# Aggregating four batches at once: 49 two-level Strassen products with a streamed right operand in place of 26 products on pairs

## The chip, the core and the metric

The kernel runs on one core of one Trainium2 chip, all in fp32. The metric is the device time of one execution in microseconds (us). Three runs of the kernel before gave 1821.66, 1821.86 and 1822.44 us, a median of 1821.86.

## What is computed

There are 16 batches of 1024 nodes with 128 features, and one 1024 x 1024 matrix `adj` that all of them share. Layer 0 is one graph convolution and layer 1 is five steps of a gated unit. Both take the normalized and rectified input and add their result to the residual.

```python
# layer 0
h = relu(layernorm(x));  x = x + adj @ (h @ W) + bias
# layer 1
h = relu(layernorm(x))
for _ in range(5):
    m  = adj @ h                       # the aggregation
    av = concat([m, m])
    u3 = h @ u3_w.T + u3_b
    z  = sigmoid(av @ w3_w.T + w3_b + u3)
    r  = sigmoid(av @ w4_w.T + w4_b + u3)
    hv = tanh(av @ w5_w.T + w5_b + (r * h) @ u5_w.T + u5_b)
    h  = (1 - z) * h + z * hv
x = x + h
```

`in_matrix` and `out_matrix` are the same matrix, so the two halves of each weight are added once and one aggregation per step is enough. The heavy parts are the aggregation (1024 x 1024 times 1024 x 128 for each batch, once in layer 0 and five times in layer 1) and the **gates** (five 128 x 128 products on 1024 columns for each batch and step).

## The kernel before

Batches go in eight **pairs**. Two pairs are in flight in layer 1, and their steps alternate: aggregation of one pair, its gates, aggregation of the other pair, its gates. While one pair is aggregated, the other's hidden state, which the gates leave transposed (features by nodes), is turned into natural order: two 32 x 32 block transposes on VectorE (`squares_to_dram`, L591), a store to DRAM (`fn<-sq`) and four loads for each batch (`natural_from`, `hN<-fn`), all issued from the SP queue (L183).

The aggregation of a pair (`aggregate`, products at L435) cuts `adj` into 4 x 4 blocks of 256 x 256 and the pair into 4 x 2 blocks. Instead of 32 block products it forms 26. Each product is two matmuls of 128x128 weights on 256 columns, since one block has two chunks of 128 nodes. The right operands of all 26 are sums of blocks of `adj`; they are made once, at the start (`adj_sums`, L279 to L284), and stay in SBUF in `right_op` for the whole program. The left operands (`forms`, L407 to L411) are sums of blocks of the pair and are made for each aggregation on VectorE and ScalarE. Products are accumulated in four PSUM banks (b1 to b4); ScalarE copies banks out (`pair_of` L447, `one_of` L452) and VectorE adds the copies into `mT`, the transposed result (L459, L462).

The layer 0 aggregations of pairs 0 and 1 are done without the scheme (`aggregate_plainly`, L554), with 512-column matmuls. The other six pairs' layer 0 work, called the prelude, runs as a background of layer 1: small pieces are put between products by `place(k)`, and the pair's aggregation takes the turn of one step. `po` (L675) is layer 0's product with W.

The gates (`gates`, L714 to L755) work on four units of 512 columns in a pair: for each unit two matmuls into a bank, a sigmoid, then a third matmul into the same bank and a second sigmoid, then two matmuls into another bank and a tanh. `pr` are the banks of the sigmoids, `pv` those of the tanh.

The order of instructions on every engine is the order in which the program is written (`pin`). DMAs all go through `dma` on SP.

Of the kernel before, what the change touches and what calls it, by code (L numbers as in the profile page):

```python
# [43 lines left out]
EARLY = (  # L44
    ("=p3", "p3"),
    ("=p2", "p2"),
    ("a3", "q3", "+", "q4"),
    ("a9", "p3", "+", "a3"),
    ("a10", "p2", "-", "a3"),
    ("a1", "q1", "-", "q3"),  # L50
    ("a7", "p3", "-", "a1"),
    ("a2", "q1", "+", "q2"),
    ("a8", "p2", "+", "a2"),
    ("a4", "q1", "+", "q4"),
    ("=q4", "q4"),
    ("a13", "p4", "+", "a9"),
)
LATE = (
    ("a6 a5", "p23", "+", "q23"),
    ("a15", "p1", "+", "a8"),  # L60
    ("a18", "p4", "+", "a15"),
    ("a16", "a18", "-", "a2"),
    ("a17", "a16", "+", "a1"),
    ("=p1", "p1"),
    ("=p4", "p4"),
    ("a19", "q4", "+", "a18"),
    ("a14", "p1", "-", "a7"),
    ("a11", "q2", "+", "a3"),
    ("a12", "a13", "+", "a10"),
)  # L70
FORM = {a: i for i, a in enumerate(" ".join(f[0] for f in EARLY + LATE).split())}

PRODUCTS = (
    ("T", "=p3", 1, 0),
    ("U", "=p2", 1, 1),
    ("V", "a9", 2, 0),
    ("W", "a10", 2, 1),
    ("X", "a3", 3, 0),
    ("R", "a7", 1, 0),
    ("S", "a8", 1, 1),  # L80
    ("D1", "a4", 4, 0),
    ("D2", "=q4", 4, 0),
    ("O", "a13", 3, 0),
    ("Y", "a1", 1, 0),
    ("Z", "a2", 1, 1),
    ("M", "a5", 2, 0),
    ("N", "a6", 2, 1),
    ("J", "a16", 4, 0),
    ("K", "a17", 1, 0),
    ("L", "a18", 1, 1),  # L90
    ("A1", "=p1", 3, 0),
    ("A2", "=p4", 3, 0),
    ("F", "a19", 4, 0),
    ("H", "a14", 1, 0),
    ("I", "a15", 1, 1),
    ("E", "a11", 2, 0),
    ("G", "=q4", 2, 1),
    ("B", "a12", 1, 0),
    ("C", "=p4", 1, 1),
)  # L100
RIGHT = {p[0]: i for i, p in enumerate(PRODUCTS)}
OPENS = {"T": 1, "V": 2, "X": 3, "D1": 4, "J": 4, "F": 4}

RIGHT_SUMS = (
    ("N", "R24", "-", "R14"),
    ("Z", "R21", "-", "R24"),
    ("T", "R31", "-", "R34"),
    ("B", "R32", "+", "R33"),
    ("G", "R44", "-", "R34"),
    ("S", "N", "-", "R21"),  # L110
    ("t0", "R13", "+", "R14"),
    ("J", "R12", "+", "t0"),
    ("t1", "R23", "+", "R24"),
    ("K", "J", "-", "t1"),
    ("H", "t1", "-", "t0"),
    ("t2", "R31", "+", "R33"),
    ("R", "H", "-", "t2"),
    ("Y", "R", "-", "R12"),
    ("t3", "R12", "+", "R32"),
    ("M", "t3", "-", "R42"),  # L120
    ("t4", "K", "+", "B"),
    ("W", "t4", "-", "R22"),
    ("O", "R42", "-", "t4"),
    ("U", "W", "+", "R21"),
    ("X", "W", "m", "R34"),
    ("V", "O", "-", "R34"),
    ("A2", "R41", "-", "O"),
    ("F", "O", "+", "R43"),
    ("L", "t1", "-", "F"),
    ("I", "R14", "-", "L"),  # L130
    ("t5", "t1", "-", "R44"),
    ("C", "R43", "-", "t5"),
    ("t6", "R11", "+", "S"),
    ("D1", "t6", "-", "R"),
    ("D2", "A2", "-", "D1"),
)
SINGLES = (("A1", 0, 0), ("E", 1, 1))
# [3 lines left out]


ANY, BLOCK, HOLD = range(3)
FREE = (6, 8, 11, 13, 17, 20, 24)
PLAIN = ((0, 0), (1, 1), (0, 1), (1, 0))
UNITS = ((1, 0), (1, 1), (0, 0), (0, 1))
# [3 lines left out]
def tile_two_gnn_layers(  # L150
# [17 lines left out]
    pairs = B // 2  # L168
# [3 lines left out]
    nat = ctx.enter_context(tc.tile_pool(name="nat", bufs=4))  # L172
    flip = ctx.enter_context(tc.tile_pool(name="flip", bufs=2))
    tr = ctx.enter_context(tc.tile_pool(name="tr", bufs=6))
    agg = ctx.enter_context(tc.tile_pool(name="agg", bufs=1))
# [15 lines left out]
    def load_x(b, xt=None, parts=((0, NC),)):  # L191
        xt = xt or x_tile(b)
        for cs in parts:
            cs = slice(*cs)
            dma(xt[:, cs], by_slots(x[b])[:, cs])
        return xt
# [8 lines left out]

    right_op = const.tile([P, len(PRODUCTS), SB, BLK], F32, tag="right", name="right_op")
    forms = const.tile([P, len(FORM), SB, D], F32, tag="forms", name="forms")


    raw = [[None] * NH for _ in range(NB)]  # L210

    def load_adj(i, g, t=None):
        if g == 0 and t is None:
            t = nat.tile([P, N], F32, tag="hN", name=f"raw_{i}")
        elif g == 1:
            first = len(FORM) - (NB - i) * 2 * SB
            t = forms[:, first : first + 2 * SB].rearrange("p s j d -> p (s j d)")
        raw[i][g] = t.rearrange("p (c n) -> p c n", c=SB)
        parts = SB if (i, g) == (0, 0) else 1
        for k in range(parts):  # L220
            cs = bass.ts(k, SB // parts)
            dma(raw[i][g][:, cs], adjT[:, bass.ts(i, SB), bass.ts(g, HALF)][:, cs])

    gb = const.tile([P, D], F32, tag="gb", name="gb")
    w_sb = const.tile([P, 9, D], F32, tag="w", name="w_sb")
    b_sb = const.tile([P, 5], F32, tag="b", name="b_sb")
    xts = {0: load_x(0, parts=((0, 2), (2, CH), (CH, NC))), 1: x_tile(1)}
# [3 lines left out]


    def other_loads(k):
        if k == 0:
            pin(nc.vector.memset(xts[1][:, 0, 0:1], 0.0))
            load_x(1, xts[1])
            load_adj(2, 0)
            return
        if k == 1:
            raw_3 = nat.tile([P, N], F32, tag="hN", name="raw_3")  # L240
            pin(nc.vector.memset(raw_3[:, 0:1], 0.0))
            load_adj(3, 0, raw_3)
            return
        first = len(FORM) - NB * 2 * SB
        pin(nc.vector.memset(forms[:, first, 0, 0:1], 0.0))
        for i in range(NB):
            load_adj(i, 1)
        for b in range(2, 4):
            xts[b] = load_x(b)
        for name, i, j in SINGLES:  # L250
            dma(right_op[:, RIGHT[name]], adjT[:, bass.ts(i, SB), bass.ts(j, BLK)])
        dma(gb, gbias.to_broadcast([P, D]))
        dma(w_sb, weights)
        dma(b_sb, biases)
# [6 lines left out]
    between = {}  # L261

    def adj_sums(first, last):
        def operand(name):
            if name in RIGHT:
                return right_op[:, RIGHT[name]]
            if name in between:
                return between[name]
            i, j = int(name[1]) - 1, int(name[2]) - 1
            return raw[i][j // 2][:, :, bass.ts(j % 2, BLK)]  # L270

        for dst, a, op, b in RIGHT_SUMS[first:last]:
            if dst not in RIGHT:
                tag = "rz"[len(between) % 2]
                t = work.tile([P, HALF], F32, tag=tag, name=f"between_{dst}")
                between[dst] = t.rearrange("p (c n) -> p c n", c=SB)
            o = operand(dst)
            if op == "+":
                pin(nc.vector.tensor_add(o, operand(a), operand(b)))  # L279
            elif op == "-":  # L280
                pin(nc.vector.tensor_sub(o, operand(a), operand(b)))
            else:
                pin(
                    nc.vector.scalar_tensor_tensor(  # L284
                        o, operand(a), -1.0, operand(b), ALU.mult, ALU.subtract
                    )
                )
# [7 lines left out]
    def weight_sums():  # L295
        for wa, wb in ((W3A, W3B), (W4A, W4B), (W5A, W5B)):
            pin(nc.vector.tensor_add(w_sb[:, wa, :], w_sb[:, wa, :], w_sb[:, wb, :]))
        pin(nc.vector.tensor_sub(w_sb[:, W3A, :], w_sb[:, W3A, :], w_sb[:, W4A, :]))
        for i, (ba, bb) in enumerate(((B3, BU3), (B4, BU3), (B5, BU5))):
            pin(nc.vector.tensor_add(bsum[:, i : i + 1], b_sb[:, ba : ba + 1], b_sb[:, bb : bb + 1]))  # L300
        pin(nc.vector.tensor_scalar_mul(nb3, bsum[:, 0:1], -1.0))

    def normalize(dst, src, nm, then, in_parts=False):

        stats, mv, ve, rstd, nmr = {}, {}, {}, {}, {}
        every, first, second = range(NC), range(CH), range(CH, NC)

        def statistics(i, cs):  # L310
            if i not in stats:
                stats[i] = small.tile([P, NC, 6], F32, tag="stats", name=f"stats_{nm}{i}")
            for c in cs:
                pin(nc.vector.bn_stats(stats[i][:, c, :], src[i][:, c, :]))

        def scales(i, cs=every):
            if i not in mv:
                mv[i] = small.tile([P, NC, 2], F32, tag="mv", name=f"mv_{nm}{i}")
                ve[i] = small.tile([P, NC], F32, tag="ve", name=f"ve_{nm}{i}")
# [629 lines left out]
    for piece in todo:  # L949
        piece()  # L950
# [39 lines left out]
```

## Time and profile before

| | before |
|---|---|
| median of three runs | 1821.86 us |
| the profiled execution | 1821.55 us |
| its span, first to last instruction | 1819.8 us |
| TensorE (PE) busy | 1812.6 us, 100% of the span |
| VectorE (DVE) busy | 1391.5 us, 76% |
| ScalarE (ACT) busy | 759.0 us, 42% |
| GpSimd (POOL) busy | 124.8 us, 7% |
| moved by DMA | 145.15 MB, 80 GB/s on average |
| mean granted TensorE clock | 1.000 |

Busy time is the time in which an engine executes an instruction. The profile counts a matmul in fp32 as two records, so 6810 records on PE are about half as many matmuls. A TensorE record's duration is modelled at its end; the spacing of two starts is the better measure of what a matmul costs. DMA-issuing instructions don't count as busy time of the engine that issues them.

### The profile page before, as it was taken

To read this page: it belongs to the slowest core of one execution; us is meant where nothing else is said; L and a number is where in the kernel's file an instruction comes from. 1 tells how busy PE (TensorE), PEld (TensorE's weight loads), DVE (VectorE), ACT (ScalarE), POOL (GpSimd) and SP (SyncE) were. 2 spreads that over 40 slices of the span, in tenths; PEclk is the share of its full clock that TensorE was granted. 3 is DMA by queue.
4 is the path that set the end of the run, shared out by engine and by line. 5 is a ranking of instruction groups with operands and counts; after the bars stand their busy time and mean duration, and the time that the engine had idled before them with its cause. 6 is when DMAs were issued, how large, how long until landed. Compare 5 with 4: busy or idle time off the path is not lost.

```text
span 1819.8 us, 20644 instructions
## 1 busy us (share of the span) xinstructions
PE 1812.6 (100%) x6810; PEld 1273.2 (70%) x6810; DVE 1391.5 (76%) x3266; ACT 759.0 (42%) x1487; POOL 124.8 (7%) x169
## 2 busy tenths in 40 slices
PE   9999999999999999999999999999999999999999
PEld 4666877677766687668766678666866677776666
DVE  6887877687788786878778877777878777766777
ACT  3445354435335334543434533553344333334433
POOL 4211002000002000200000200020000000000000
PEclk9999999999999999999999999999999999999999
DMA  4231132112631113111352111311153312111123
GB/s 165 88 121 47 47 92 71 46 47 76 196 111 58 47 47 116 47 47 47 112 178 93 58 58 36 116 47 55 39 160 106 105 58 75 54 46 47 47 70 116
DMA packets 87803, 145.15 MB, mean 80 GB/s; under 512 B 9744, under 2 KB 65168, under 8 KB 87696
## 3 DMA queue, kind: packets, MB, share of 16 engines
q1 hardware_dynamic: 87696, 143.83, 25.1%
q8 instruction: 54, 0.88, 0.2%
q14 instruction: 53, 0.43, 0.1%
HBM read 77.73 MB, written 66.06 MB: 79 GB/s over the span
## 4 chain that ended last, share of the span: by engine, by line
PE 98%; DVE 2%; DMA 0%; issue 0%; ACT 0%; DVEq 0%
PE pr L714 23%; PE bT L435 22%; PE pv L714 15%; PE bV L435 11%; PE bX L435 7%; PE bD L435 4%; PE bT_a L435 3%; PE pq_a L554 3%; PE bJ L435 2%; PE bF L435 2%; PE bV_a L435 2%; PE po L675 2%; PE bX_a L435 1%; PE bD_a L435 1%; DMA raw<-in_adjT_dram 0%; PE bJ_a L435 0%
## 5 line engine op out<-in xcount | busy, mean ns | idle before, releaser
L435 PE MATMUL bT<-right_op,forms 128*128 128x256 f32 x1920 | 455.0, 379 | 0.0
L435 PEld LDWEIGHTS bT<-right_op,forms 128*128 128x128 f32 x1920 | 364.4, 190 | 64.0 <-issue 8.4
L714 PE MATMUL pr<-mT,w_sb 128*128 128x512 f32 x640 | 307.4, 593 | 0.3 <-DVE mT L462 0.3
L435 PE MATMUL bV<-right_op,forms 128*128 128x256 f32 x960 | 228.0, 379 | 0.0
L714 PEld LDWEIGHTS pr<-mT,w_sb 128*128 128x128 f32 x640 | 121.7, 190 | 136.4 <-issue 132.3
L726 ACT ACTIVATE r<-pr,bsum 128x512 f32<-128x512 f32 x160 | 109.8, 686 | 246.4 <-PE pr L714 246.1
L727 DVE TENSOR_TENSOR r<-r,hT 128x512 f32<-128x512 f32 x160 | 110.7, 692 | 127.3 <-ACT r L726 125.5
L435 PEld LDWEIGHTS bV<-right_op,forms 128*128 128x128 f32 x960 | 181.6, 190 | 23.9
L749 ACT ACTIVATE hv<-pv,bsum 128x512 f32<-128x512 f32 (+1 forms) x161 | 110.3, 685 | 163.8 <-PE pv L714 163.8
L714 PE MATMUL pv<-r,w_sb 128*128 128x512 f32 (+1 forms) x322 | 163.6, 590 | 0.0
L714 PE MATMUL pv<-mT,w_sb 128*128 128x512 f32 (+1 forms) x322 | 163.6, 590 | 0.0
L714 PE MATMUL pr<-hT,w_sb 128*128 128x512 f32 x320 | 163.5, 593 | 0.0
L753 DVE TENSOR_TENSOR hv<-hv,hT 128x512 f32<-128x512 f32 x156 | 105.8, 678 | 73.6 <-ACT hv L749 73.6
L435 PE MATMUL bX<-right_op,forms 128*128 128x256 f32 x640 | 157.8, 379 | 0.0
L435 PEld LDWEIGHTS bX<-right_op,forms 128*128 128x128 f32 x640 | 121.2, 190 | 16.0
L755 DVE TENSOR_TENSOR hT<-hT,hv 128x512 f32<-128x512 f32 (+1 forms) x161 | 110.9, 689 | 16.7 <-PE pv L714 0.5
L734 ACT ACTIVATE z<-pr,bsum 128x512 f32<-128x512 f32 x160 | 110.1, 688 | 20.2 <-PE pr L714 20.2
L714 PEld LDWEIGHTS pv<-r,w_sb 128*128 128x128 f32 x322 | 61.3, 190 | 76.1 <-issue 61.9
L714 PEld LDWEIGHTS pr<-hT,w_sb 128*128 128x128 f32 x320 | 60.9, 190 | 76.5 <-issue 76.5
L714 PEld LDWEIGHTS pv<-mT,w_sb 128*128 128x128 f32 x322 | 61.1, 190 | 76.0 <-issue 75.5
L754 DVE TENSOR_TENSOR hv<-hv,z 128x512 f32<-128x512 f32 x156 | 107.9, 692 | 5.4
L591 DVE STREAM_TRANSPOSE sq<-hT 128x512 f32<-128x512 f32 x156 | 101.3, 688 | 0.0
(176 smaller groups left out, 2277.0 us busy)
## 6 DMA issues: line engine op xcount, KB each, us to landing
fn<-sq SPq DMA_DIRECT2D x78, 512.0 KB, 2.9
hN<-fn SPq DMA_DIRECT2D x312, 128.0 KB, 3.5
ft<-hP_b SPq DMA_DIRECT2D x64, 128.0 KB, 2.4
x1d<-xt SPq DMA_DIRECT2D x16, 512.0 KB, 3.2
sqt<-ft SPq DMA_DIRECT2D x16, 512.0 KB, 6.1
x<-x1d SPq DMA_DIRECT2D x16, 512.0 KB, 5.2
xt<-in_x_dram SPq DMA_DIRECT2D x15, 512.0 KB, 6.2
out_dram<-x SPq DMA_DIRECT2D x14, 512.0 KB, 2.8
```

Of the source, the lines that this page charges most:

```text
L435: nc.tensor.matmul(halves(bank)[:, half], forms[:, FORM[form], c, :], right_op[:, RIGHT[name], c, :], start=bool(opens) and c == 0, stop=c ...
L554: nc.tensor.matmul(bank, hN[i][:, c, :], raw[c // SB][g][:, c % SB], start=c == 0, stop=c == NC - 1,)
L591: pin(nc.vector.transpose(squares_of_half(sq, g), transposed_half(hT, g)))
L675: nc.tensor.matmul(pt[:, j, :], aT[i][:, bass.ts(g * CH + j, P)], w_sb[:, WG, :], start=True, stop=True,)
L714: nc.tensor.matmul(bank, w_sb[:, w, :], moving, start=start, stop=stop, skip_group_check=True)
L726: pin(nc.scalar.activation(r, pg, AF.Sigmoid, bias=bsum[:, 1:2]))
L727: pin(nc.vector.tensor_mul(r, r, view(hT, u)))
L734: pin(nc.scalar.activation(z[u], banks[u], AF.Sigmoid, bias=bsum[:, 0:1]))
L749: pin(nc.scalar.activation(hv, pg, AF.Tanh, bias=bsum[:, 2:3]))
L753: pin(nc.vector.tensor_sub(hv, hv, h))
L754: pin(nc.vector.tensor_mul(hv, hv, z[u][:, part]))
L755: pin(nc.vector.tensor_add(h, h, hv))
```

## The change

Batches go in four **quads**; two quads are in flight in layer 1 and their steps alternate as the pairs did. The aggregation of a quad is a 2 x 2 Strassen product (in Winograd's form) with seven big products, each of them again a 2 x 2 Strassen product with seven small ones: 49 small products. A small product has a 256 x 256 right operand and 128 feature columns of weights, so it is again two matmuls of 128x128 weights on 256 columns.

What goes with it:

- **Right operands.** 49 blocks don't fit beside the rest. Ten are kept in SBUF (`RESIDENT`); the other 39 are sums written to DRAM at the start, or plain blocks of `adj`, and each aggregation reads them through a ring of twelve 256 KB buffers. The read for the product twelve streamed products ahead is issued from **ScalarE's queue**, after the copy that ends a product.
- **Bank copies.** Each of the 49 products is copied out of PSUM by ScalarE on its own (128 x 256). Where a product accumulates onto an earlier one in the same bank (1, then 6, 7, 4; and 5, then 3), the copy lies between the two.
- **Left operands** are made in two levels: seven big ones from natural order in four rotating rooms (`big`), and four sums for each big product (`little`, two buffers). VectorE adds the copies of a big product and then, by `level`, the big products (1024 columns in one instruction).
- **Layer 0.** The first eight batches (two quads) are now aggregated plainly; two quads remain as background.
- **Gates.** A quad's gates are two runs of the same function, A and B, one after the other, on two batches each.
- One `nat` tile holds the natural order of the next quad. It is loaded in the second half of an aggregation, after products 24 and 31.

Cut to its core:

```diff
-EARLY = (
...
-PRODUCTS = (
-    ("T", "=p3", 1, 0),
...
-RIGHT_SUMS = (
...
+BIG = (1, 2, 6, 5, 7, 3, 4)
+def _small_products():
+    order = []
+    for i in range(NBIG):
+        more = i + 1 < NBIG
+        order += [(i, 6), (i, 5)] + [(i + 1, 1)] * more + [(i, 7), (i, 3)] + [(i + 1, 2)] * more
+        order += [(i, 4)]
...
+RESIDENT = [(i, 7) for i in range(NBIG)] + [(i, 5) for i in (1, 3, 5)]
+STREAM = [k for k in SMALL if k not in RESIDENT]
+RING = 12
...
+FREE = range(2, NSMALL, 2)
...
-    right_op = const.tile([P, len(PRODUCTS), SB, BLK], F32, tag="right", name="right_op")
-    forms = const.tile([P, len(FORM), SB, D], F32, tag="forms", name="forms")
+    big = const.tile([P, 4, 2, CH, D], F32, tag="big", name="big")
+    little = const.tile([P, 2, 4, SB, D], F32, tag="little", name="little")
+    ring = const.tile([P, RING, SB, BLK], F32, tag="ring", name="ring")
+    resident = const.tile([P, len(RESIDENT), SB, BLK], F32, tag="resident", name="resident")
+    nat = const.tile([P, Q, NSQ, NC, SQ], F32, tag="nat", name="nat")
...
+    def stream():
+        n = streamed[0]
+        if n == aggregations * len(STREAM):
+            return
+        streamed[0] += 1
+        key = STREAM[n % len(STREAM)]
+        i, p = key
+        if key in parked_right:
+            src = parked_right[key]
+        else:
...
+            src = adjT[:, bass.ts(2 * a + c, SB), bass.ts(2 * b + d, BLK)]
+        pin(nc.scalar.dma_start(out=ring[:, n % RING], in_=src))
...
+        level = {
+            0: [],
+            1: [(result(0, 0), X, home[1])],
+            2: [(X, X, home[2])],
+            3: [],
+            4: [(result(1, 0), X, home[4]), (result(1, 1), result(1, 0), Y), (X, X, Y)],
+            5: [(X, X, home[5])],
+            6: [(result(1, 0), result(1, 0), home[6])],
+        }
...
+        def multiply(i, p):
+            tag = {2: "b", 5: "c", 3: "c"}.get(p, "a")
+            opens = p in (1, 2, 5)
...
+            if (i, p) in RESIDENT:
+                right = resident[:, RESIDENT.index((i, p))]
+            else:
+                right = ring[:, (n * len(STREAM) + STREAM.index((i, p))) % RING]
+            for c, l in enumerate(left(i, p)):
+                pin(
+                    nc.tensor.matmul(
+                        bank,
+                        l,
+                        right[:, c, :],
+                        start=opens and c == 0,
...
+            pin(nc.scalar.copy(to, bank))
+            if (i, p) in STREAM:
+                stream()
+            if p == 3:
+                add(z[:, 0], z[:, 0], flat(v[:, 0:2]))
+            elif p == 4:
+                add(z[:, 1, BLK:], z[:, 1, BLK:], v[:, 2])
+                for o, a, b in level[i]:
+                    add(o, a, b)
...
+        for a, key in enumerate("AB"):
+            pair = slice(2 * a, 2 * a + 2)
...
+            gates(
+                [mT[:, 2 * a + k] for k in range(2)],
+                hT[pair],
...
+    aggregate_plainly([s for s, _ in firsts], "a0", place)
...
+    aggregate_plainly([s for s, _ in seconds], "a1", place)
+    for _ in range(RING):
+        stream()
+    po(2 * Q - 1, 1)
```

In the notation (i, p) of the diff, i counts the big product in the order of `BIG` and p is the small product's number. A bank of tag "a" has two buffers, "b" and "c" have one each.

## The prediction

> **What bounds the kernel now.** First the page's part on busy time and the chain of work that ended last, then that chain in order of time over one step, which is where the prices come from.
>
> ```profile
> PE 1812.6 (100%) x6810; PEld 1273.2 (70%) x6810; DVE 1391.5 (76%) x3266; ACT 759.0 (42%) x1487; POOL 124.8 (7%) x169
> PE 98%; DVE 2%; DMA 0%; issue 0%; ACT 0%; DVEq 0%
> ...
> 278.22 10.30 PE pr L714 x24
> 288.52 6.87 PE pv L714 x16
> 317.84 10.30 PE pr L714 x24
> ...
> 401.44 0.89 PE po L675 x8
> ```
>
> TensorE is never idle for long, and the chain stays on it for 98% of the span. So the time is the number of matmuls times their spacing. The chain gives the spacing (start, length, and two records for each matmul): 12 gate matmuls in 10.30 us, 0.858 us for 512 columns; from 288.52 + 6.87 = 295.39 to 317.84 lie a pair's 52 product matmuls, 0.4317 us each; four `po` matmuls take 0.89 us.
>
> Do the counts reproduce the span? 46 pair aggregations (40 steps, 6 preludes) x 52 x 0.4317 = 1032.6; 800 gate matmuls and 64 plain ones x 0.858 = 741.6; 128 `po` and 16 of the ending x 0.223 = 32. That is 1806.3 of 1819.8; the 13.5 us left are start, end and small gaps. The model holds.
>
> The other engines, in a stretch without background work, then the DMA queue's waits, its issues, and two seconds of a burst of `hN<-fn` loads (columns: PE, PEld, DVE, ACT, POOL busy, clock, DMA share, GB/s):
>
> ```profile
> 1500.00:1600.00 100.00, 100.00 (x379) 71.58 (x378) 71.56 (x150) 36.21 (x69) 0.00 (x0) 1.00 0.19 59
> 568.00:569.00 1.00, 1.00 (x6) 0.90 (x5) 1.00 (x5) 0.14 (x1) 0.00 (x0) 1.00 0.93 228
> 570.00:571.00 1.00, 1.00 (x6) 0.89 (x5) 1.00 (x7) 0.68 (x2) 0.00 (x0) 1.00 0.92 207
> ```
>
> ```profile
> SPq L183 <- DMA sqt<-ft: 19.3, 11, 2.6
> 10.75 1.91 SPq L183 DMA_DIRECT2D forms<-in_adjT_dram  x4
> 302.43 4.24 SPq L183 DMA_DIRECT2D hN<-fn  x8
> hN<-fn SPq DMA_DIRECT2D x312, 128.0 KB, 3.5
> sqt<-ft SPq DMA_DIRECT2D x16, 512.0 KB, 6.1
> q1 hardware_dynamic: 87696, 143.83, 25.1%
> ```
>
> DVE and ACT have room. The DMA engines are a quarter used, but a burst of 1 KB rows already fills them (share 0.92) at 207 to 228 GB/s. One issue holds SP's queue for 1.91/4 = 0.48 us or 4.24/8 = 0.53 us; a simple one took 0.34. A landing takes 3.5 us, 6.1 where many are in flight.
>
> **What the Trainium skill says.** *Perfetto Trace Analysis*, "DMA Instruction — HWDGE": the issuing sequencer is free for its next instruction only when the descriptors are generated, and a semaphore wait happens on that sequencer first. The 0.34 to 0.53 us agree; that ACT pays the same is not shown, since it issues nothing here. *DMA: Bandwidth & Descriptors*, "Issuing engines are not separate DMA queues": ACT's transfers will share the 16 engines with SP's. No run here shows it. *PSUM — Partial Sum Buffer*, "The four PSUM rules": a partial sum may be read in the middle of an accumulation group if it is synchronised. The trace agrees: L726 reads `pr` before L714's third matmul adds to it, with no wait on PE.
>
> **The change, part by part.**
>
> *Products.* A quad takes 98 matmuls of 256 columns where two pairs took 104. The built program holds 22 x 98 = 2156 of them; 2392 go. Saved: 236 x 0.4317 = 101.9 us.
>
> *Plain aggregation* now covers eight batches: 64 more matmuls x 0.858 = +54.9 us. Gates, `po` and the ending keep their counts.
>
> PE's sum: 1806.3 - 101.9 + 54.9 = 1759.3; with the same 13.5 us around it a span of 1772.8. The profiled execution was 1.75 us longer than its span and 0.3 below the median, so **1774.6 us** if nothing waits.
>
> *VectorE.* A quad's aggregation has 35 adds of 256 columns (0.42), 15 of 512 (0.69) and 7 of 1024 (no row; the line through the two gives 1.23): 33.7 us, and gates and transposes 8 x (4 x 0.69 + 0.65) = 27.3. Rows overlap: the same count for a pair's step gives 32.0 us, the window above 71.56% of 39.61 = 28.3, so rows count 0.89. That makes 54 us in a step of 76.7, the 71% of before. Not on the path on average. But DVE ends gates some 6 us late already (its rows run to 341.6 after PE left them at 335), and background norms (about 3.6 us each, three to an aggregation) bring it to 44 us in 42.4. A second small left operand is wanted 5 products (4.3 us) after it is put, and the copy of (6,1) needs big product 4's first add, 0.9 us ahead. I take 1 us for each of seven aggregations with norms; bounds 0 and 3.
>
> *ScalarE.* 49 copies x 0.373 (the `one_of` row) = 18.3 us in 42.4, and 39 issues: 30 simple ones x 0.34 + 9 in two runs x 0.48 = 14.5. Sum 33 us if issue and copy don't overlap, 0.71 for a streamed product of 0.863. It fits; below, at no overlap with SP's issues in the way, it doesn't. A copy has slack: two products (1.73 us) lie between uses of a bank, less the 0.43 of the copy and 0.2 of hand-over, **1.1 us**. Behind each issue waits the next product's copy, and behind that PE.
>
> *The ring's DMAs.* 22 x 39 x 262 KB = 225 MB more. An issue on ACT doesn't only wait for its buffer: the built program gives DMAs of both queues eight completion semaphores in turn, and each issue waits until the eighth before it has landed. The `sqt<-ft` line is such a wait on SP (19.3 us in all, harmless there). From product 22 to 49 an ordinary aggregation issues 23 ring reads and 16 `nat` loads in 23.3 us, 0.60 us each, so eight cover a landing of 4.8 us. In bytes: 16 reads x 0.75 + 7 with 1 KB runs x 1.0 + 16 x 0.53 = 28.5 us of DMA time (estimates between the 389 GB/s of the first loads and the 207 to 228 here), less the last eight, which needn't have landed: 22.7 in 23.3. It fits narrowly. I take 0.3 us an aggregation; bounds 0 and 5.
>
> *Crowded aggregations.* Three also carry outputs (16 loads of `ho`, residual loads, stores): 84, 78 and 57 DMAs. The first is some 53 us of DMA time in 42. Part of the excess shifts into gates, where ACT has slack. I take 5, 3 and 0 us; bounds 0 and 20 together.
>
> *Start and SP.* The ring can first be filled after the last plain product's copy, because it held the sums until then; the first small product waits about 2.7 us for issue and landing, of which four `po` cover 0.9: +2.5. The norms of the second quad all fall into the first aggregation: +3 (0 to 8). SP's moved loads (`nat`, after products 24 and 31) have half an aggregation to land: 0. The stores of right operands lie under 120 us of plain products: 0.
>
> Sum: 1774.6 + 7 + 0.3 x 19 + 8 + 2.5 + 3 = 1800.8, with each item at its more cautious middle; some overlap (a stall of PE lets DVE and DMA catch up), for which I take off 5: **1796 us**, 1.4% less.
>
> **Rivals.**
>
> 1. *PE unhindered.* Ring and DVE keep up everywhere but at the start: 1774.6 + 2.5 = 1777. For it: 25% DMA use now, and gates of 34 us in which the ring refills. Against: the 207 to 228 GB/s.
> 2. *The gain is eaten.* Items at two thirds of their upper bounds: 7 x 2 + 19 x 1 + 13 + 2.5 + 5 = 54, which is 1828 minus catch-up of 5 to 10: 1818 to 1823, nothing to measure. A difference under 0.2% (3.6 us) can't be told from none.
> 3. *ACT's queue is the bound; slower.* In products 22 to 49 each issue waits for the eighth before it. With landings of 5.7 us (between the 3.5 and 6.1 above) 39 DMAs take 39 x 5.7/8 = 27.8 us, 4.5 more than PE, less 1.1 of slack: 3.4 us x 22 = 75, so 1850 us. It decides from 47/22 = 2.1 us a time, landings of 5.4 us. For it: saturated bursts, and SP's issues holding descriptor generation too. Against: a ring read has 2 KB rows, and SP's loads can run ahead.
>
> That the change doesn't reduce the matmuls is excluded by the built program; that a product's matmuls run slower for their waits would show as spacing above 0.4317.
>
> **How the numbers follow.** My forecast (1785 to 1812) 0.50, rival 1 0.10, nearly eaten but faster (to 1818) 0.07, same 0.08, rival 3 0.25. Faster by over 0.2%: 0.67. The range takes the first four and the near part of rival 3, to break-even and 17 us beyond: 1774 to 1838; the likeliest case alone is 1785 to 1812.
>
> **What would show it.** Right: PE still about 98% of the chain, 0.43 us a product matmul, 4312 records of 256 columns in aggregations, waits of PE on ACT copies in the aggregations with outputs, on DVE in those with norms, one gap of 2 to 3 us before the first small product. Wrong: PE waiting on ACT copies in ordinary aggregations, with ACT's queue waiting on DMAs from product 22 on; a DMA share near 1 there; a granted clock below 1; or VectorE rows in the chain for more than 3%.

## The result and the profile after

| | before | after |
|---|---|---|
| median of the runs beside each other | 1822.03 us | 2042.68 us |
| profiled span | 1819.8 us | 2033.8 us |
| mean granted TensorE clock | 1.000 | 0.967 |

The changed kernel is **slower**: the ratio is 1.1214, 95% interval 1.117 to 1.1258. The forecast was 1796 us, faster than before; it was wrong in sign, and 2042.68 lies far outside its range. What is missing is 2042.7 - 1796 = 247 us.

First the page of the changed kernel: busy time of each engine, then the shares of the chain that ended last.

```profile
PE 1841.3 (91%) x6466; PEld 1223.1 (60%) x6466; DVE 1360.5 (67%) x2777; ACT 895.9 (44%) x1969; POOL 131.9 (6%) x169
...
PE 56%; DMA 27%; DVE 10%; ACT 3%; issue 2%; ACTq 1%; POOL 1%; SPq 1%; DVEq 0%; POOLq 0%
```

The matmuls went as the diff promised (6810 records to 6466), but PE is idle for 9% of the span and carries 56% of the chain in place of 98%. No other engine is near full: VectorE has less to do than before, ScalarE is at 44% (42% before). Time has gone into waits of PE, and into slow running after them: the same 6466 records keep PE busy for 1841.3 us here and for 1772.6 us in e8 below, where it hardly waits; a mean granted clock of 0.967 over 2033.8 us accounts for 67 us. These are PE's longest waits in total, by what released them (us in total, times, longest):

```profile
PE c L489 <- ACT taps L508: 59.6, 34, 5.5
PE a L489 <- DVE little L216: 59.0, 9, 14.4
PE a L489 <- ACT Z L508: 18.7, 26, 2.5
PE a L489 <- ACT mT L508: 16.7, 5, 7.6
```

Two kinds: PE waits for a bank that ScalarE has not yet copied out (`taps`, `Z`, `mT`: 95 us), and for a small left operand that VectorE has not yet made (`little`: 59 us, in only nine places).

**Where in the program.** The PE timeline gives the length of each of the 22 four-batch aggregations, from its first product to the first gate matmul. 98 matmuls x 0.4317 us make 42.31 us; the rest is **excess**. Sums of the excess in us over three classes: ten ordinary aggregations, nine with norms and their loads in the background, three with outputs in the background.

```
                                   ordinary (10)   norms (9)   outputs (3)    all
after                                   48.5         115.7        88.8       253.0
after, ring reads left out (e1)          0.6          78.8        30.5       109.9
```

That is where the missing time lies: the gates take 34.33 us a step in the changed kernel, as priced (some 3 us more in all), and the first small product comes at 135.7 us, as it does without reads and background (135.1 in e8).

**An ordinary aggregation.** The chain of the changed kernel near the end of one of them, in order of time (start, length, piece):

```profile
1537.48 4.92 DMA ring<-rd
...
1542.43 5.92 DMA ring<-rd
...
1548.36 0.03 SPq L108
...
1548.42 8.31 DMA nat<-fn
...
1556.75 0.35 ACTq L291
...
1557.19 0.38 ACT taps L508
...
1557.62 1.53 PE c L489 x4
1559.15 1.71 PE a L489 x4
```

Read from the bottom: the matmuls at 1557.62 wait for a copy of `taps`; the copy stands in ScalarE's queue behind a ring read (ACTq L291); the read waits for a `nat` load to land, which was issued by SyncE when a ring read before it had landed. Transfers release transfers, because the program gives the DMAs of both queues eight completion semaphores in turn, and each issue waits until the DMA that had its semaphore before has landed. The timeline of ScalarE at the same place (start, length, in brackets the idle time before):

```profile
1552.71 0.37 ACT L508 COPY Z<-a 128x256 f32<-128x256 f32 x1
1556.75 0.35 ACTq L291 DMA_DIRECT2D ring<-rd  x1
1557.19 0.37 ACT L508 COPY taps<-c 128x256 f32<-128x256 f32 x1 [4.11 <-DMA nat<-fn]
```

ScalarE does nothing for 4.11 us with a bank full and ready. This is what rival 3 described.

### The profile page after: what moved, and what is told of

It is laid out like the page before. It is cut to its first block, busy times and chain, and to the rows that moved or that the text cites. A ratio compares the mean times of both kernels' runs of the same rounds, so it can differ in the third digit from the quotient of the medians.

```text
span 2033.8 us, 21805 instructions
## 1 busy us (share of the span) xinstructions
PE 1841.3 (91%) x6466; PEld 1223.1 (60%) x6466; DVE 1360.5 (67%) x2777; ACT 895.9 (44%) x1969; POOL 131.9 (6%) x169
## 4 chain that ended last, share of the span: by engine, by line
PE 56%; DMA 27%; DVE 10%; ACT 3%; issue 2%; ACTq 1%; POOL 1%; SPq 1%; DVEq 0%; POOLq 0%
PE a L489 11%; DMA ring<-rd 10%; DMA nat<-fn 7%; PE c L489 6%; PE pq_a L532 3%; DMA ring<-in_adjT_dram 3%; PE b L489 2%; PE pr_1A L743 2%; PE pr_2A L743 2%; PE pr_2B L743 2%; PE pr_1B L743 2%; PE pr_3A L743 2%; PE pr_4A L743 2%; PE pr_0B L743 2%; PE pr_3B L743 2%; DMA sqt<-ft 2%
## 5 line engine op out<-in xcount | busy, mean ns | idle before, releaser
L489 PE MATMUL a<-ring,big 128*128 128x256 f32 x1120 | 304.0, 396 | 33.9 <-ACT mT L508 16.3
L508 ACT COPY Z<-a 128x256 f32<-128x256 f32 x480 | 177.1, 371 | 303.3 <-PE a L489 211.8
L489 PE MATMUL c<-ring,little 128*128 128x256 f32 x880 | 242.2, 400 | 70.2 <-ACT taps L508 59.2
L219 DVE TENSOR_TENSOR Z<-Z,taps 128x512 f32<-128x512 f32 (+1 forms) x264 | 146.2, 560 | 205.2 <-ACT taps L508 205.2
L489 PEld LDWEIGHTS a<-ring,big 128*128 128x128 f32 x1120 | 218.1, 198 | 86.4 <-ACT Z L508 29.2
L489 PEld LDWEIGHTS c<-ring,little 128*128 128x128 f32 x880 | 169.8, 198 | 111.4 <-ACT taps L508 76.0
L219 DVE TENSOR_TENSOR mT<-mT,Z 128x1024 f32<-128x1024 f32 x154 | 187.4, 1229 | 62.7 <-ACT Z L508 56.8
L489 PE MATMUL a<-ring,little 128*128 128x256 f32 x560 | 155.0, 402 | 59.8 <-DVE little L216 50.3
L489 PE MATMUL a<-resident,little 128*128 128x256 f32 x560 | 148.8, 389 | 12.3 <-DVE little L216 8.7
L489 PE MATMUL b<-ring,big 128*128 128x256 f32 x560 | 144.9, 382 | 0.0
L489 PEld LDWEIGHTS a<-resident,little 128*128 128x128 f32 x560 | 107.5, 195 | 35.0 <-issue 10.5
L508 ACT COPY taps<-b 128x256 f32<-128x256 f32 x140 | 51.9, 371 | 78.8 <-PE b L489 39.9
```

The source lines that it names most:

```text
L219: pin(nc.vector.tensor_add(o, a, b))
L489: nc.tensor.matmul(bank, l, right[:, c, :], start=opens and c == 0, stop=c == SB - 1, skip_group_check=True,)
L508: pin(nc.scalar.copy(to, bank))
```

## The experiments

Each kernel is the changed one with the edit shown (cut); ratios are to the kernel before, on the same chip, with 95% intervals. Theories are named in the expectations: Q, the ring reads in ScalarE's queue; B, the bytes of the ring; C, work elsewhere; later A, D and M for three parts of the background.

### Which part of it is the ring, and which is its queue

**e1_no_reads**

```diff
 def stream():
-        if n == aggregations * len(STREAM):
+        if n == RING:
```

> Left out: all ring reads after the first twelve; every aggregation multiplies by whatever those twelve hold. Nothing else is changed. Theory Q (the reads hold ScalarE's queue, since each waits for the eighth DMA before it, and the bank copies stand behind them): an ordinary aggregation falls from 47.7 us to 42.3, and the whole to 1775 to 1810 us. Theory B (DMA throughput: the 16 engines can't deliver the second half's bytes in time): the same numbers. Theory C (the new arithmetic itself, its copies and its VectorE adds, doesn't keep up with TensorE): stays above 1950 us, with waits on VectorE and ScalarE in place.

1893.21 us, ratio 1.0392 (1.0362 to 1.0422). It hit no expectation: the reads are worth about 150 us, and an excess of about 110 remains without them. The ten ordinary aggregations are cured (0.6 us in all); the remainder lies in the twelve with background work.

**e2_pool_reads, e3_sp_reads, e4_half_reads**: the same reads from another queue, or half their bytes in ScalarE's.

```diff
-        pin(nc.scalar.dma_start(out=ring[:, n % RING], in_=src))
+        pin(nc.gpsimd.dma_start(out=ring[:, n % RING], in_=src))   # e2
+        dma(ring[:, n % RING], src)                                # e3, SyncE
+        part = slice(0, SB) if n < RING else slice(n % SB, n % SB + 1)   # e4
+        pin(nc.scalar.dma_start(out=ring[:, n % RING][:, part], in_=src[:, part]))
```

> The same ring reads, issued from GpSimd's queue, which is nearly empty, in place of ScalarE's; GpSimd's DMAs have completion semaphores of their own, so SP's keep the eight to themselves. Theory Q: ScalarE is free, ordinary aggregations near 42.5 us, whole 1790 to 1870 us. Theory B: the bytes are the same, so ordinary aggregations stay at 46 to 50 us and TensorE now waits on the ring's DMAs; whole 1990 us or more.

1972.02 us (two runs, 1961.6 and 1982.4), ratio 1.0825 (1.069 to 1.096): between the two ranges.

> The same ring reads, issued from SP's queue in program order with all other DMAs; the eight semaphores stay shared, ScalarE is free. Theory Q, if ScalarE's queue is what matters: below 1950 us, ordinary aggregations 42 to 45 us. If the eight semaphores matter and not whose queue waits: 2000 us or more, with TensorE waiting on ring reads that stand on SP behind nat loads. Theory B: 2000 us or more and a DMA share near 1 in second halves.

1943.62 us, ratio 1.0669 (1.0638 to 1.07): in Q's range.

> Each ring read after the first twelve moves one of a buffer's two chunks of 128 rows, so half of the bytes in as many DMAs with as many waits; the other chunk holds older data. Theory B: the second half of an aggregation needs 5.1 MB in place of 8.1 in 23.3 us, far below what the engines move, so ordinary aggregations fall to 42.3 to 43 us and the whole to 1780 to 1850. Theory Q in the form that the number of DMAs in flight sets the pace whatever their size: landings stay at 4 us or more, ordinary aggregations stay at 45 us or more, whole above 1930.

1940.58 us, ratio 1.0652 (1.0621 to 1.0683): the whole is above B's range, but the ordinary aggregations, at 42.5 us, are where B put them.

Excess over the ten ordinary aggregations: 2.1 us on SyncE, 1.6 with half the bytes, 10.5 on GpSimd (all of it in the first three), 48.5 in the changed kernel. So ScalarE's queue is needed for the cost, as Q says. e3 has the same bytes and the same eight semaphores in turn. The queue's waits of SyncE, in one such aggregation of e3, show the waits still there:

```profile
SPq L108 <- DMA ring<-rd: 6.0, 10, 1.1
...
SPq L108 <- DMA nat<-fn: 1.1, 4, 0.5
```

and the list of PE's waits in the same 42.3 us is empty. Nor were the DMA engines idle there; the same stretch of e3 by windows (PE, PEld, DVE, ACT, POOL busy, clock, DMA share, GB/s):

```profile
1537.20:1546.70 9.50, 9.50 (x45) 8.37 (x44) 8.19 (x17) 4.09 (x11) 0.00 (x0) 1.00 1.03 373
1546.70:1556.20 9.50, 9.50 (x46) 8.37 (x45) 5.94 (x13) 5.10 (x13) 0.00 (x0) 1.00 1.07 295
```

Share 1, PE without a gap: full DMA engines alone cost PE nothing here. But e4 shows that they have a part. From product 22 to the end of the aggregation shown above, with a DMA share of 1.03, the changed kernel's transfers landed after (last figure, median us)

```profile
ring<-rd ACTq DMA_DIRECT2D x14, 256.0 KB, 5.2
ring<-in_adjT_dram ACTq DMA_DIRECT2D x7, 256.0 KB, 6.4
nat<-fn SPq DMA_DIRECT2D x13, 128.0 KB, 5.6
```

and those of e4, in the same part of the same aggregation, with a share of 0.75, after

```profile
ring<-rd ACTq DMA_DIRECT2D x14, 128.0 KB, 2.8
nat<-fn SPq DMA_DIRECT2D x13, 128.0 KB, 3.5
ring<-in_adjT_dram ACTq DMA_DIRECT2D x7, 128.0 KB, 3.1
```

Eight issues cover a landing of 4.8 us, by the prediction's count; the first three lines are above it, the last three below. The cost takes both, landings longer than the eight cover and a queue in which PE's bank copies stand behind the wait. Taking away either one (e4, e3) cures it.

### What the background costs

**e5_relu_alone** (on e3): the background's relus take constants.

```diff
-                        bias=self.nmr[:, c : c + 1],
-                        scale=self.rstd[:, c : c + 1],
+                        bias=self.nmr[:, c : c + 1] if not self.plain else mhalf[:, c : c + 1],
+                        scale=self.rstd[:, c : c + 1] if not self.plain else 1.0,
```

> Ring reads are issued by SyncE as in e3 (1943.6 us), and the background norms' relus take constants as scale and bias (so those batches are not normalised): they no longer wait, on ScalarE's queue, for VectorE's shift and GpSimd's power. Theory A (background relus waiting on ScalarE's queue hold the bank copies): the nine aggregations with norms shrink from an excess of about 93 us to under 50, the time is 1885 to 1905 us. Theory D (VectorE standing for its own DMAs makes the small left operands late): at most 15 us fall, 1928 or more. Theory M (the background's transfers themselves fill the DMA engines): no change, 1938 to 1948.

1911.13 us, ratio 1.0501 (1.0463 to 1.0539). 32.5 us below e3, more than D (VectorE standing for its own loads) allowed and 6 short of A (the background's relus holding ScalarE's queue). The nine aggregations with norms fell from 91.7 to 57.9 us of excess; the others stayed.

**e8_no_bg_compute** (on e1): besides, the background's relus take constants as in e5, and its statistics, scales, shift and output adds on VectorE are left out (the four norms of the first aggregation keep theirs).

```diff
-            box["n"].statistics(range(CH))
-            lambda: box["n"].statistics(range(CH, NC)),
-            lambda: box["n"].scales(EVERY),
-                    norm.shift(EVERY)
-                add(x1[:, :, js], x1[:, :, js], box["h"][:, :, js])
```

> Ring reads left out as in e1 (1893.2 us), and of the background also what VectorE does (statistics, scales, shift, output adds) and the wait of its relus (constants as scale and bias); the relus themselves and all transfers of the background stay. Theories A and D together (engine queues held by background work): the 110 us of excess in twelve aggregations fall to under 30, 1785 to 1812 us. Theory M (the transfers): 1860 us or more.

1795.28 us, ratio 0.9854 (0.9838 to 0.987). All but 13.6 us of excess are gone, while the background's transfers and its relus still run. Its page:

```profile
PE 1772.6 (99%) x6466; PEld 1203.2 (67%) x6466; DVE 1309.7 (73%) x2465; ACT 886.2 (49%) x1969; POOL 106.2 (6%) x153
```

VectorE is 49 us less busy than in e1 (1359.1). That is half of the 98 us between the two kernels, on an engine that is idle for more than a quarter of the span; so at least half is waits and what follows from them. PE's slow running after waits is part of it: the mean granted clock is 0.982 in e1 and 1.000 in e8, some 34 us. One aggregation of e1 with a norm shows the waits. PE's, ScalarE's and VectorE's waits in that window:

```profile
PE c L489 <- ACT taps L508: 5.5, 1, 5.5
```

```profile
ACT hb L348 <- DVE nmr_b L335: 9.4, 2, 6.5
```

```profile
DVE stats_a L318 <- DMA xt<-in_x_dram: 3.3, 1, 3.3
```

A relu of the background stands on ScalarE for 6.5 us, waiting for a shift which VectorE has not reached; behind it stands the copy of `taps`, and PE 5.5 us. On VectorE statistics wait for a load of x, with left operands and level adds behind them.

**e6_out_add_on_pool, e7_shift_and_add_on_pool** (on e3): can another engine take the waiting?

```diff
-                add(x1[:, :, js], x1[:, :, js], box["h"][:, :, js])
+                pin(nc.gpsimd.tensor_add(x1[:, :, js], x1[:, :, js], box["h"][:, :, js]))
 # e7 besides: shift as two products on GpSimd, right behind the power
+            pin(nc.gpsimd.tensor_tensor(nmr, self.mv[:, part, 0], self.rstd[:, part], ALU.mult))
+            pin(nc.gpsimd.tensor_tensor(nmr, nmr, mone[:, part], ALU.mult))
```

> Ring reads are issued by SyncE as in e3, and the adds of the outputs go to GpSimd instead of VectorE, nothing left out. Theory D: the three aggregations with outputs (excess 66 us in e3) lose most of it, and the time falls by 35 to 60 us, to 1885 to 1910. Theory M: ring and natural loads stay late there, fall of under 12 us, 1932 or more. Theory A says nothing of these three: no change.

1942.73 us, ratio 1.0659 (1.0643 to 1.0675): no change, the three aggregations with outputs at 66.8 us of excess (65.9 in e3). D fails for them, in the presence of the reads. The wait went elsewhere; PE's waits, of e6:

```profile
PE c L489 <- DMA ring<-rd: 17.9, 10, 4.3
...
PE a L489 <- DMA ring<-rd: 14.9, 10, 2.9
...
PE a L489 <- DVE little L216: 8.2, 4, 2.5
```

In e3 `little` was 32.4 us and `ring<-rd` 6.2 (3.6 before `a`, 2.6 before `c`).

> As e6_out_add_on_pool, and the background norms' shift is also computed by GpSimd, right behind its power and three pieces (not two) ahead of the first relu, so that neither VectorE's queue nor a GpSimd round trip stands between. Theory A: another 25 to 45 us below e6_out_add_on_pool. Theory D or M: within 10 us of it.

1961.56 us, ratio 1.0759 (1.0739 to 1.0779), 19 us worse than e6, but not cleanly to be read: the edit also reaches the norms of the start, where the first small product came at 159.0 us in place of 133.5. In the aggregations alone the excess fell by 11.4 us (162.0 to 150.6), at the edge of what D and M (the transfers themselves) allow, and far from A's 25 to 45.

### Reads and background taken apart, and three queues compared

**e9_sp_reads_no_bg, e10_act_reads_no_bg, e12_pool_reads_no_bg**: e8 with all ring reads, from SyncE, ScalarE and GpSimd.

```diff
-        if n == RING:
+        if n == aggregations * len(STREAM):
-        pin(nc.scalar.dma_start(out=ring[:, n % RING], in_=src))     # stays in e10
+        dma(ring[:, n % RING], src)                                  # e9
+        pin(nc.gpsimd.dma_start(out=ring[:, n % RING], in_=src))     # e12
```

> As e8_no_bg_compute (VectorE's part of the background and the waits of its relus left out), but with the ring reads, issued by SyncE. If what the reads cost on SyncE is the filled DMA engines in the crowded aggregations (50 us between e1 and e3), it stays: 1830 to 1848 us. If it came from background work that was already waiting, little is left: 1797 to 1810 us.

1908.0 us, ratio 1.0475 (1.0453 to 1.0498): some 60 us above both ranges.

> As e9_sp_reads_no_bg, but the reads are issued by ScalarE as in the changed kernel. If ScalarE's queue alone costs what the ten ordinary aggregations of the changed kernel show (4.85 us) wherever natural loads and reads meet, all 22 have it and the crowded three more: 1900 to 1930 us. If the two causes only add up (2042.7 - 98): 1935 to 1955 us. If reads on ScalarE hurt only beside background work there: under 1870 us.

1916.72 us, ratio 1.0521 (1.0498 to 1.0544): in the first range. The 22 aggregations are 45 to 52 us long, and those with outputs hardly longer than the rest.

> As e9 and e10 (VectorE's part of the background and the waits of its relus left out), with the ring reads issued by GpSimd, whose queue then holds only them, the bias adds and a few powers. If queue order is what the reads cost (on SyncE behind loads and stores that wait, on ScalarE ahead of the bank copies): 1797 to 1820 us. If the DMA engines are full with these bytes: 1860 us or more, the crowded aggregations above 50 us each.

1828.29 us, ratio 1.0035 (1.0022 to 1.0048): 8 us above the range for queue order and 32 below that for bytes.

The three move the same bytes. What SyncE's queue adds is seen in the chain of e9, in its aggregation with the first outputs:

```profile
1100.21 5.11 DMA ho<-fn
...
1105.99 7.21 DMA ho<-fn
...
1113.21 5.71 DMA nat<-ft
...
1118.98 6.10 DMA ring<-rd
...
1125.22 2.04 PE a L490 x4
```

A ring read, wanted by PE, comes after a chain of output and natural loads. That aggregation took 63.3 us in e9 and 47.1 in e12. Yet the DMA engines of e12 were as full in it:

```profile
1048.00:1058.00 10.00, 9.90 (x45) 8.11 (x44) 9.76 (x18) 5.11 (x13) 4.61 (x8) 1.00 1.02 314
1058.00:1068.00 10.00, 10.00 (x48) 8.81 (x47) 7.04 (x14) 4.29 (x12) 5.52 (x10) 1.00 1.07 276
```

Share 1 again, PE full. Part of e12's wait has only moved, though: behind the second aggregation with outputs its gates take 45.9 us in place of 34.3, since a copy out of `nat`, whose loads come late, stands in ScalarE's queue ahead of a sigmoid (PE waits 8.6 us for `r_0A`).

*DMA: Bandwidth & Descriptors*, "Queues, rings and completion order", in the Trainium skill, says that each engine takes turns between the queues that have work; a read in a queue of its own then needn't wait for all that was issued ahead of it. e9 and e12 agree with that; the turns themselves no run here shows. There is a second difference: in e9 the reads share eight completion semaphores with SyncE's other DMAs, in e12 they have eight of their own. The two were not separated.

So the two causes stand in a small table (medians, us; rows e8 to e10, e12 and e1 to e3, after):

```
                       no reads   on GpSimd   on SyncE   on ScalarE
background computed     1893.2      1972.0     1943.6      2042.7
left out                1795.3      1828.3     1908.0      1916.7
```

The way from the floor to the changed kernel: 1795.3 + 97.9 (background alone) + 121.4 (reads on ScalarE alone) + 28.1 (both together) = 2042.7. Where the last term arises was not traced, and its sign holds for ScalarE's queue, not in general: on GpSimd the reads cost 33.0 us without the background's computing and 78.8 with it, on SyncE 112.7 and 50.4.

### Does a mended version beat the kernel before?

**e11_bg_on_pool** (on e3): scaling, relu and output adds on GpSimd, x loaded earlier, outputs spread.

```diff
-                norm.relu(range(2 * k, 2 * k + 2))
+                    pin(nc.gpsimd.tensor_scalar(dst, src, mean, rstd, ALU.subtract, ALU.mult))
+                    pin(nc.gpsimd.tensor_scalar_max(dst, dst, 0.0))
-            todo.extend(two_by_two(outs))
+                todo.extend([(a, True)] + [(None, False)] * gap + [(b, False)])
```

> A mended version, nothing left out: ring reads issued by SyncE, the background norms' scaling and relu and the output adds computed by GpSimd (so that neither ScalarE's nor VectorE's queue waits for them), x loaded two pieces earlier and outputs spread over more aggregations. If the queues held by background work are the cause: aggregations with norms at 43 to 46 us in place of 48 to 61, crowded ones at 43 to 50, 1815 to 1850 us. If GpSimd's work slows VectorE's (the adds then being longer than 0.42 us) or the DMA engines are the limit: 1870 us or more.

1971.04 us, ratio 1.0806 (1.0781 to 1.083), 27 us worse than e3 and in the upper range. ScalarE and VectorE were freed of that work, and SyncE's queue took their place. Its waits and PE's, in e11:

```profile
SPq L108 <- POOL ha L684: 41.4, 6, 15.9
```

```profile
PE c L489 <- DMA ring<-rd: 67.7, 24, 7.5
```

The stores of the slower norms wait at the head of SyncE's queue, with the ring reads behind.

**e13_pool_reads_bg_spaced, e14_spaced_half_reads**: reads on GpSimd, and the waits of the background moved apart in time; e14 with half the bytes.

```diff
+            put(now[0] + 1, lambda: box["n"].statistics(range(CH, NC)))
             lambda: box["n"].scales(EVERY),
+            lambda: box["n"].shift(EVERY),          # a piece of its own
-                    norm.shift(EVERY)               # ahead of the first relu
-            todo.extend(two_by_two(outs))           # outputs: 8 free pieces between load and add
+                todo.extend([(a, True)] + [(None, False)] * gap + [(b, False)])
```

> A mended version, nothing left out: reads issued by GpSimd, the background norms' statistics one product apart, their shift a piece of its own two products behind the power and two ahead of the first relu, outputs with eight free pieces between load and add. If it is waits in ScalarE's and VectorE's queues that cost: below e2_pool_reads (1972) by 80 us or more, 1850 to 1890. If the DMA engines are full: 1920 us or more, PE waiting for the ring or VectorE for its loads.

1884.83 us, ratio 1.0349 (1.0331 to 1.0367): in the range for waits. Against e2 (the same queue, not spaced; its two runs lie 21 us apart) 87 us are gained by order alone.

> As e13_pool_reads_bg_spaced, but each ring read after the first twelve moves one of its two chunks (the other chunk of the right operand is the one that stood there before). If bytes are what is left: 40 us or more below e13. If order and waits: within 20 us of it.

1850.13 us, ratio 1.0154 (1.0139 to 1.0169). 34.7 us for half of the bytes: between the two expectations, so bytes have a share here.

**e15_spaced_further, e16_adj_blocks_copied** (on e13).

```diff
-            pieces.append((lambda b=b: bias(b), False))
+            pieces.append((lambda b=b: bias_on_dve(b), False))     # two adds of 512 on VectorE
-    pieces = [load(bs[0]), load(bs[1]), (None, False)]
+    pieces = [load(bs[0]), load(bs[1])] + [(None, False)] * (3 if quad == 2 else 6)
 # e16 besides
+            store_right((i, p), raw[2 * a + c][b][:, :, bass.ts(d, BLK)])
```

> As e13_pool_reads_bg_spaced, nothing left out, with the bias adds moved from GpSimd (ahead of ring reads in its queue) to VectorE in two adds of 512 columns, x loaded up to five pieces earlier, the last quad's outputs two pieces further apart and the norms of the first aggregation spaced like the others. If waits in queues are what is left: 30 to 55 us below e13 (1884.8), 1830 to 1855. If the DMA engines are: less than 15 below it.

1860.01 us, ratio 1.0217 (1.02 to 1.0234): 24.8 us below e13, between the two expectations; in its 22 aggregations 36.7 us went (100.2 to 63.5), but 8 us came in gates, where PE waited 5.8 us for `mT`.

> As e15_spaced_further, but the nine blocks that the ring reads from adjT in 1 KB rows are first stored to DRAM as the sums are, and read in 2 KB rows. If short rows make reads late: 5 to 15 us below e15. If the ring is far enough ahead with them: within 4 us.

1861.9 us, ratio 1.022 (1.0205 to 1.0236): no difference to e15. Rows of 1 KB for nine of 39 reads cost nothing that can be measured.

No version that computes everything beats the kernel before. e15 takes back 183 of the 247 us; 63.5 us of excess are left in its aggregations. PE's longest waits there are 20.7 us for left operands that come late (`little`) and 11.3 for copies to `mT`. Whether a better order removes them is open.

## Why the prediction was wrong

**Right.** The counts and PE's prices. e8 runs at 42.36 us an ordinary aggregation and 34.33 us a step's gates, and ends at 1795.3 us, 18 above the 1777 of rival 1 (13.6 of them excess in the aggregations). 225 MB of ring traffic, VectorE's lower share and the start were near. That the kernel nearly without waits gives the number that was forecast, 1796, is chance: the forecast had put 21 us of waits into it. One sum slipped without effect: the product and plain terms come to 1774.9, not 1774.6.

All four signs that the prediction named for being wrong came: PE waiting for copies in ordinary aggregations, a DMA share near 1 there, a clock below 1, and VectorE at 10% of the chain.

**Wrong, the step "The ring's DMAs".** It took 0.3 us for each of 19 aggregations, since 22.7 us of DMA time in 23.3 "fits narrowly" (its three terms make 27.5 and not 28.5, so 21.7; that slip isn't what failed). The measure was the bytes between two points of time, and they fit, or can come late without harm: e3 reads the ring from SyncE's queue, and its aggregation takes 42.3 us with PE never waiting. But a queue that must not stop is not served by a mean that fits: each issue waits for one landing, the eighth before it. Eight cover 4.8 us; the medians above were 5.2 to 6.4, and the `nat` load at the end took 8.31. Measured: 4.85 us in each ordinary aggregation, 5.7 on average in all 22 of e10 (126.0 / 22).

**Rival 3 had this mechanism and its place**, and priced it at 3.4 us a time; the pause shown above is 3.8 us (the product before started at 1552.95, ended 4 x 0.216 later, and the next starts at 1557.62). It left out that PE did not start again at full speed: the eight records after the pause took 1.53 + 1.71 = 3.24 us in place of 1.73. Together 5.3 us. The granted clock of these two stretches, 0.69 and 0.50, is the third figure from the end:

```profile
1557.62:1559.15 1.53, 1.53 (x5) 1.30 (x6) 0.00 (x0) 0.37 (x1) 0.00 (x0) 0.69 0.86 245
1559.15:1560.86 1.71, 1.71 (x5) 1.33 (x5) 1.03 (x2) 0.37 (x1) 0.00 (x0) 0.50 0.62 196
```

The rival's 75 us in all compare with 121.4 for the reads on ScalarE alone. It had a chance of 0.25, too low on the numbers at hand: rival 3 and the forecast differed in whether eight cover a landing of 4.8 or of 5.7 us, and the landings that it knew were 3.5 and 6.1.

**Wrong, the step "VectorE"** (1 us for each of seven aggregations, measured 115.7 us in nine, 78.8 without the reads) **and the start's "+3"** (the first of the nine, 7.1 us, still inside its bounds). It summed VectorE's busy time, 44 us in 42.4; taking 49 us of that work away in e8 took 98 us off the time. What was missing is that the background's pieces wait, on in-order queues, for another engine or a transfer; no rival priced such waits either. With the work itself they make the 109.9 us of excess in e1. The profile before had these waits. ScalarE's of the kernel before:

```profile
ACT hP_a L339 <- DVE nmr_a L331: 21.8, 12, 4.3
...
ACT hP_b L339 <- DVE nmr_b L331: 1.9, 1, 1.9
```

There 23.7 us of such waits cost PE nothing. In e1 they are 59.7 us (31.4 for `ha`, 28.3 for `hb`), up to 7.7 us at a time, and PE waits behind them. Why PE could afford them before was not tried; for the changed kernel the prediction itself puts the slack of a copy at 1.1 us.

**Wrong, the step "Crowded aggregations"** (5, 3 and 0 us). Measured 88.8 us. 30.5 of it is there without any reads (VectorE's adds waiting for their loads). The assumption that part of the excess of transfers shifts into gates holds once nothing is computed behind the loads: these three have 19.6 us in e10 and 4.8 in e12. But it isn't free there: the gates behind the second of them take 39.9 and 45.9 us in place of 34.3. With the reads on SyncE behind those loads (e9), 59.7 us are left in the three.

**"Off 5 for overlap"** had the wrong sign: with the reads on ScalarE the two causes cost 28 us more together than one by one.

## What to carry to other kernels

Price a new DMA by the queue that issues it: what waits ahead of it, for how long at worst, and what stands behind it; compare that with the slack of what stands behind, not mean traffic with mean time. A queue that feeds the bounding engine (here the bank copies on ScalarE) should hold nothing that can wait long for a third party, neither a DMA issue nor a background operation whose operand another engine still has to make; move the wait to a queue on which nobody depends, and place producer and consumer of background work several pieces apart. Before a change that shortens the slack, list the waits that the profile shows and that cost nothing: they are the ones that come onto the path.

## What the runs showed of the hardware

- **The issuing engine was worth 88 us with the same bytes** (1916.7 on ScalarE, 1908.0 on SyncE, 1828.3 on GpSimd). The Trainium skill, *DMA: Bandwidth & Descriptors*, "Issuing engines are not separate DMA queues", says that another issuer saves only the time of issuing. Here GpSimd's issue is the dearest and its landing no shorter. The group of its issues on the page of e2 (busy us, mean ns of one), then the part on DMA issues (median us to landing):

```profile
L291 POOL DMA_DIRECT2D ring<-rd x660 | 359.0, 545 | 1009.9 <-PE a L489 749.3
```

```profile
ring<-rd POOLq DMA_DIRECT2D x660, 256.0 KB, 5.8
```

  ScalarE's took 0.35 us and landed in 5.1 (median over the changed kernel). What differs is who waits in which queue, and for GpSimd the set of completion semaphores too. The order of the three is not fixed: with the background computed it is 2042.7, 1943.6 and 1972.0.
- **A DMA share of 1 is no rate.** The four windows above have it at 276 to 373 GB/s, and PE is busy for all but 0.1 us of them.
- **A pause of PE can cost more than itself.** After 3.8 us without work the next eight records took 3.24 us for 1.73, at a granted clock down to 0.50. Not every pause did: after one of 2.8 us, before 1723.50 in the same profile, eight records took 1.83 us at a clock of 1.00. The mean granted clock was 0.967 in the changed kernel and 1.000 in e8.
